# Second tile's normalisation interleaved with the first tile's, in an RWKV block on one core

## The chip, the core and the metric

The kernel runs on one core of one Trainium2 chip. The metric is the device time of one execution in microseconds. A core has engines that each work through their own instructions in order: TensorE (PE, with its weight loads PEld), VectorE (DVE), ScalarE (ACT), GpSimd (POOL) and SyncE (SP). DMA transfers are issued from the queues of SP, ACT and POOL. Engines wait for each other on semaphores.

## The reference

The input x is 2 sequences of 4096 positions with 256 features, float32. The block has two halves, each on a layer norm of x and each added to x:

```python
# attention half (RWKV), on n = layernorm(x); n_prev is n moved by one position
xk, xv, xr = (n * mix + n_prev * (1 - mix) for mix in (mix_k, mix_v, mix_r))
k, v, r = xk @ W_k.T, xv @ W_v.T, sigmoid(xr @ W_r.T)
# a recurrence over positions: running log-max p, numerator q, decay w, bonus u
new_p = max(p, u + k_t)
wkv_t = (exp(p - new_p) * q + exp(u + k_t - new_p) * v_t) / (the two exponentials' sum)
x = x + (r * wkv) @ W_o.T
# feed-forward half, on n = layernorm(x); weights are -1, 0 or 1 with a scale per output
h = silu(n @ w1.T * s1) * (n @ w2.T * s2)
h = gelu(h @ h1.T * sh1)
h = gelu(h @ h2.T * sh2)
x = x + h @ w3.T * s3
```

Layer norm here is (x - mean) / sqrt(variance + 1e-5) over the 256 features.

## The kernel before

Features lie on the 128 partitions, in two halves `h`; positions run along the free axis. A tile is 512 positions, so there are 16 tiles, 8 for each sequence. Tile 0 alone is cut into two pieces of 256 positions (`parts(i)`), so that its steps overlap.

A tile passes through three Python generators, each of which yields between its steps:

- `normalise(i)`: takes the tile's input `x_sb` from `loaded`, starts the load of the next tile on POOL's queue (`load_x`), and runs the first layer norm into `xn`.
- `attention(i)`: mixes `xn` with its neighbour into three tiles `mx`; for each half `h` forms the products `ps_k`, `ps_v`, `ps_r` in PSUM and runs the recurrence `wkv` on VectorE and ScalarE, with the result in `y`; forms the output products `ps_o` and adds them into `x_sb`; runs the second layer norm into `x2`; splits it into a rounded part `x2_hi` and a rest `x2_lo`.
- `ffn(i)`: the feed-forward half. Each product is done twice, with the rounded part and with the rest (`split_product`). The first layer's products are `pa` and `pb`, the next two layers' `ph`, the last one's `po`.

`layernorm` sums the two halves into `both`, takes the mean over partitions with a product against a constant matrix (`average`, into PSUM tile `mean`), subtracts it, squares on ScalarE, takes the variance in the same way (`var`), takes the root on ScalarE and the reciprocal on VectorE, and multiplies. For tile 0 `average` is one float32 product. For the others (`busy`) the sum is first split, with a copy on ScalarE and a subtraction on VectorE into `sums`, and two products are done.

The loops at the end set the order: tile 0 goes through `normalise` and `attention` alone, then `normalise(1)` stands whole; after that the steps of `ffn(i)` are interleaved with those of `attention(i + 1)` and `normalise(i + 2)`:

```python
    run(normalise(0))
    run(attention(0))
    run(normalise(1))
```

A scheduler then orders the instructions of each engine from this; pools give the buffers (`ps_attn` has three PSUM buffers, `ps_sum` one, `ps_ffn` four). ScalarE holds one set of function tables at a time; a change of function can need a table load, which the profile shows as ACT_TABLE_LOAD.

At the start the weights are loaded: `vec` and `wa_sb` (the attention's) on SP's queue, behind half of tile 0's input; the other half of it on ACT's; the feed-forward weights on POOL's, where `w1`, `w2`, `h1`, eight pieces of `h2` (through memory, `h2_hbm`) and `w3` follow each other, and then the input of tile 1. When all tiles are done, a flag decides whether a general version of the block is needed; with these inputs it isn't.

Of the kernel before, what the change touches and what calls it, by code (L numbers as in the profile page):

```python
# [12 lines left out]
P = 128  # L13
B, T, D, HID = 2, 4096, 256, 1024
TS = 512
# [47 lines left out]
def split_block(ctx, tc, flags, x, vecs, w_attn, w1, w2, h1, h2, w3, out):  # L63
# [26 lines left out]

    def load_x(i):
        x_sb = xpool.tile([P, ND, TS], F32, tag="x", name="x_sb")
        for p, queue in zip(parts(i), (nc.sync, nc.scalar) if i == 0 else (nc.gpsimd,)):
            queue.dma_start(out=x_sb[:, :, p], in_=hbm(x, *tiles[i])[:, :, p])
        return x_sb

    loaded = {0: load_x(0)}
    vec = const.tile([P, NVEC], F32, name="vec")
    nc.sync.dma_start(out=vec, in_=vecs)
    wa_sb = const.tile([P, 4, ND, D], F32, name="wa_sb")  # L100
# [11 lines left out]
        nc.gpsimd.dma_start(out=h2_hbm[f], in_=h2[:, :, f * P : (f + 1) * P])  # L112
    nc.gpsimd.dma_start(out=w3_sb, in_=w3)

    mean_w = const.tile([P, P], F32, name="mean_w")
    vector.memset(mean_w, 1.0 / D)
    mean_wr = const.tile([P, P], F32R, name="mean_wr")
    scalar.activation(mean_wr, mean_w, AF.Copy)
    eps = const.tile([P, 1], F32, name="eps")
    vector.memset(eps, LN_EPS)  # L120
    unmix = const.tile([P, 3 * ND], F32, name="unmix")
    vector.tensor_scalar(unmix, vec[:, 0 : 3 * ND], -1.0, 1.0, ALU.mult, ALU.add)

# [30 lines left out]
    def split_product(psum, weights, src):  # L154

        n = len(src)
        for c in range(n):
            hi, lo = src[c]
            tensor.matmul(psum, weights(c), hi, start=c == 0, stop=False)  # L159
            tensor.matmul(psum, weights(c), lo, start=False, stop=c == n - 1)  # L160

    def split(hi, lo, full):

        scalar.activation(hi, full, AF.Copy)  # L164
        vector.tensor_tensor(lo, full, hi.bitcast(F32), ALU.subtract)  # L165

    def average(psum, both, busy):

        if busy:
            pieces = one.tile([P, 2, TS], F32R, tag="sums", name="sums")  # L170
            split(pieces[:, 0, :], pieces[:, 1, :], both)
            split_product(psum, lambda c: mean_wr, [(pieces[:, 0, :], pieces[:, 1, :])])
        else:
            tensor.matmul(psum, mean_w, both, start=True, stop=True)

    def layernorm(src, xc, tag, parts, busy):


        both = one.tile([P, TS], F32, tag=tag, name="both")
        mean = ps_sum.tile([P, TS], F32, tag="ps", name="mean")  # L180
        for p in parts:
            vector.tensor_tensor(both[:, p], src[:, 0, p], src[:, 1, p], ALU.add)
            average(mean[:, p], both[:, p], busy)
        for p in parts:
            for h in range(ND):
                vector.tensor_tensor(xc[:, h, p], src[:, h, p], mean[:, p], ALU.subtract)
        yield
        sq = wide.tile([P, ND, TS], F32, tag="wide", name="sq")
        var = ps_sum.tile([P, TS], F32, tag="ps", name="var")
        rstd = one.tile([P, TS], F32, tag=tag, name="rstd")  # L190
        for p in parts:
            scalar.activation(sq[:, :, p], xc[:, :, p], AF.Square)
            vector.tensor_tensor(sq[:, 0, p], sq[:, 0, p], sq[:, 1, p], ALU.add)
            average(var[:, p], sq[:, 0, p], busy)
        for p in parts:
            scalar.activation(rstd[:, p], var[:, p], AF.Sqrt, bias=eps)  # L196
        yield
        for p in parts:
            vector.reciprocal(rstd[:, p], rstd[:, p])  # L199
            for h in range(ND):  # L200
                vector.tensor_tensor(xc[:, h, p], xc[:, h, p], rstd[:, p], ALU.mult)
        yield

    def wkv(h, k, v, r, y, parts, first):

        w, u = col(DECAY, h), col(FIRST, h)

        lm = one.tile([P, TS + 1], F32, tag="lm", name="lm")
        num = one.tile([P, TS + 1], F32, tag="num", name="num")
        if first:  # L210
            vector.memset(lm[:, 0:1], LOG_ZERO)
            vector.memset(num[:, 0:1], 0.0)  # L212
        else:
            vector.tensor_copy(lm[:, 0:1], log_max[:, h : h + 1])
            vector.tensor_copy(num[:, 0:1], numer[:, h : h + 1])

        def after(p):
            return slice(p.start + 1, p.stop + 1)

        sc = one.tile([P, 2, TS], F32, tag="sc", name="sc")


        so = one.tile([P, 2, TS], F32, tag="so", name="so")
        for p in parts:
            vector.tensor_tensor_scan(
                lm[:, after(p)], w.to_broadcast([P, p.stop - p.start]), k[:, p], lm[:, p.start : p.start + 1],
                ALU.add, ALU.max,
            )  # L230
            vector.scalar_tensor_tensor(sc[:, 1, p], lm[:, p], w, k[:, p], ALU.add, ALU.subtract)
            vector.tensor_scalar(sc[:, 0, p], sc[:, 1, p], NEG_CLAMP, 0.0, ALU.max, ALU.min)
            vector.tensor_scalar(sc[:, 1, p], sc[:, 1, p], 0.0, -NEG_CLAMP, ALU.max, ALU.min)
            scalar.activation(sc[:, 0, p], sc[:, 0, p], AF.Exp)
            scalar.activation(sc[:, 1, p], sc[:, 1, p], AF.Exp, scale=-1.0)
            vector.scalar_tensor_tensor(so[:, 1, p], k[:, p], u, lm[:, p], ALU.add, ALU.subtract)
            vector.tensor_scalar(so[:, 1, p], so[:, 1, p], NEG_CLAMP, -NEG_CLAMP, ALU.max, ALU.min)
        vector.tensor_copy(log_max[:, h : h + 1], lm[:, TS:])
        for p in parts:
            scalar.activation(so[:, 0, p], so[:, 1, p], AF.Sigmoid, scale=-1.0)  # L240
            scalar.activation(so[:, 1, p], so[:, 1, p], AF.Sigmoid)
            scalar.activation(r[:, p], r[:, p], AF.Sigmoid)
        yield
        for p in parts:
            vector.tensor_tensor(sc[:, 1, p], sc[:, 1, p], v[:, p], ALU.mult)
            vector.tensor_tensor_scan(
                num[:, after(p)], sc[:, 0, p], sc[:, 1, p], num[:, p.start : p.start + 1], ALU.mult, ALU.add
            )
        vector.tensor_copy(numer[:, h : h + 1], num[:, TS:])
        yield  # L250
        for p in parts:
            vector.tensor_tensor(so[:, 0, p], so[:, 0, p], num[:, p], ALU.mult)
            vector.tensor_tensor(so[:, 1, p], so[:, 1, p], v[:, p], ALU.mult)
            vector.tensor_tensor(so[:, 0, p], so[:, 0, p], so[:, 1, p], ALU.add)
            vector.tensor_tensor(y[:, h, p], so[:, 0, p], r[:, p], ALU.mult)
        yield
# [3 lines left out]
    def normalise(i):  # L260

        x_sb = loaded.pop(i)
        if i + 1 < len(tiles):
            loaded[i + 1] = load_x(i + 1)

        xn = one.tile([P, ND, TS + 1], F32, tag="xn", name="xn")
        if tiles[i][1] == 0:
            vector.memset(xn[:, :, 0:1], 0.0)
        else:
            vector.tensor_copy(xn[:, :, 0:1], prev)  # L270
        yield from layernorm(x_sb, xn[:, :, 1:], "rstd1", parts(i), i > 0)
        vector.tensor_copy(prev, xn[:, :, TS:])
        normal[i] = (x_sb, xn)

    def attention(i):
# [21 lines left out]
        for h in range(ND):  # L297
            kvr = []
            for m, name in enumerate("kvr"):
                ps = ps_attn.tile([P, TS], F32, tag="pa", name="ps_" + name)  # L300
                for p in ps_of:
                    product(
                        ps[:, p],
                        lambda c, m=m: wa_sb[:, m, c, h * P : (h + 1) * P],
                        [mixed[m][:, c, p] for c in range(ND)],
                    )
                kvr.append(ps)
            yield
            yield from wkv(h, *kvr, y, ps_of, first)

        for h in range(ND):
            ps = ps_attn.tile([P, TS], F32, tag="pa", name="ps_o")
            for p in ps_of:
# [4 lines left out]
                )  # L318
                vector.tensor_tensor(x_sb[:, h, p], x_sb[:, h, p], ps[:, p], ALU.add)
        yield  # L320
        x2 = wide.tile([P, ND, TS], F32, tag="wide", name="x2")
        yield from layernorm(x_sb, x2, "rstd2", ps_of, i > 0)
        x2_hi = one.tile([P, ND, TS], F32R, tag="x2_hi", name="x2_hi")
        x2_lo = one.tile([P, ND, TS], F32R, tag="x2_lo", name="x2_lo")
        for p in ps_of:
# [58 lines left out]
        for _ in steps:  # L384
            pass

    normal, got = {}, {}
    run(normalise(0))
    run(attention(0))
    run(normalise(1))  # L390
    for i in range(len(tiles)):
        ahead = attention(i + 1) if i + 1 < len(tiles) else iter(())
        further = normalise(i + 2) if i + 2 < len(tiles) else iter(())
        for step, _ in enumerate(ffn(i, *got.pop(i))):

            if step >= NH:
                next(ahead, None)
            if step > 2 * NH - 2 and step % 2:
                next(further, None)
        run(ahead)  # L400
        run(further)
# [287 lines left out]
```

## Time and profile before

| | |
|---|---|
| runs, device us | 1613.01, 1613.53, 1614.44; median 1613.53 |
| profiled execution, device us | 1613.69 |
| its span | 1611.9 us |
| around the span | 1.8 us |
| mean granted TensorE clock | 0.993 |
| busy: PE / DVE / ACT / POOL | 1571.8 / 1077.4 / 1014.0 / 58.4 us |

The profile records one execution. "Busy" is the time in which an engine has an instruction in work; a row of the timeline gives an instruction's start and length in microseconds, its engine, its line in the kernel, what it writes and reads, and in brackets how long the engine had stood idle before it and what it then had waited for. The clock is the share of TensorE's full speed that was granted. A line can be that of a helper: all split products have lines 159 and 160, all plain products 152.

### The profile page before, as it was taken

To read this page: it belongs to the slowest core of one execution; us is meant where nothing else is said; L and a number is where in the kernel's file an instruction comes from. 1 tells how busy PE (TensorE), PEld (TensorE's weight loads), DVE (VectorE), ACT (ScalarE), POOL (GpSimd) and SP (SyncE) were. 2 spreads that over 40 slices of the span, in tenths; PEclk is the share of its full clock that TensorE was granted. 3 is DMA by queue.
4 is the path that set the end of the run, shared out by engine and by line. 5 is a ranking of instruction groups with operands and counts; after the bars stand their busy time and mean duration, and the time that the engine had idled before them with its cause. 6 is when DMAs were issued, how large, how long until landed. Compare 5 with 4: busy or idle time off the path is not lost.

```text
span 1611.9 us, 16567 instructions
## 1 busy us (share of the span) xinstructions
PE 1571.8 (98%) x6314; PEld 1189.0 (74%) x6314; DVE 1077.4 (67%) x1746; ACT 1014.0 (63%) x1351; POOL 58.4 (4%) x91
## 2 busy tenths in 40 slices
PE   4799999999999999999999999999999999999997
PEld 3577778777777777777777777777778777787786
DVE  7767667585766958668585676857668575675521
ACT  6566666766657567576666657667576666657542
POOL 2000000000000000000000000000000000000000
PEclk9899999999999999999999999999999999999999
DMA  9003122130311203113030221203112031110202
GB/s 366 26 1 105 40 79 72 33 116 15 105 53 53 92 14 118 39 52 99 19 119 27 78 72 43 96 13 102 43 53 85 7 105 40 65 59 34 91 9 72
DMA packets 36230, 109.16 MB, mean 68 GB/s; under 512 B 3632, under 2 KB 12336, under 8 KB 35504
## 3 DMA queue, kind: packets, MB, share of 16 engines
q1 hardware_dynamic: 18992, 68.45, 13.0%
q0 software_dynamic: 16880, 39.33, 7.9%
q8 instruction: 51, 0.84, 0.2%
q14 instruction: 35, 0.29, 0.1%
q10 hardware_dynamic: 272, 0.26, 0.0%
HBM read 99.64 MB, written 12.58 MB: 70 GB/s over the span
## 4 chain that ended last, share of the span: by engine, by line
PE 79%; issue 15%; DMA 3%; DVE 1%; ACT 1%; POOL 0%; POOLq 0%; ACTq 0%
PE ph L159 24%; PE ph L160 24%; PE pa L159 3%; PE pa L160 3%; PE pb L159 3%; PE pb L160 3%; PE po L159 3%; PE po L160 3%; PE ps_o L152 3%; PE ps_v L152 3%; PE ps_r L152 3%; PE ps_k L152 3%; DMA h_hbm<-in_h 1%; DMA x_sb<-in_x 1%; PE mean L159 0%
## 5 line engine op out<-in xcount | busy, mean ns | idle before, releaser
L159 PE MATMUL ph<-hi,h_sb 128*128 128x512 f32 x2048 | 817.2, 399 | 0.3 <-DMA h_sb<-h_hbm 0.3
L160 PE MATMUL ph<-lo,h_sb 128*128 128x512 f32 x2048 | 803.7, 393 | 0.0
L159 PEld LDWEIGHTS ph<-hi,h_sb 128*128 128x128 f32 x2048 | 384.6, 188 | 95.4 <-issue 7.4
L160 PEld LDWEIGHTS ph<-lo,h_sb 128*128 128x128 f32 x2048 | 385.0, 188 | 90.8 <-issue 7.2
L365 DVE TENSOR_TENSOR lo<-full,hi 128x512 fp32r<-128x512 f32 x256 | 175.3, 685 | 321.7 <-ACT full L364 321.6
L362 ACT ACTIVATE hi<-ph,vec 128x512 fp32r<-128x512 f32 x256 | 176.0, 687 | 295.5 <-PE ph L160 294.4
L364 ACT ACTIVATE full<-ph,vec 128x512 f32<-128x512 f32 x256 | 174.3, 681 | 0.0
L362 ACT ACT_TABLE_LOAD x102 | 130.9, 1283 | 1.8
L346 ACT ACTIVATE gated<-pa,vec 128x512 f32<-128x512 f32 x128 | 86.9, 683 | 63.5 <-PE pa L160 62.3
L347 DVE SCALAR_TENSOR_TENSOR gated<-pb,vec,gated 128x512 f32<-128x512 f32 x128 | 95.4, 748 | 31.3 <-PE pb L160 21.9
L199 DVE RECIPROCAL rstd<-rstd 128x512 f32<-128x512 f32 (+1 forms) x34 | 107.2, 3158 | 6.9 <-ACT rstd L196 6.9
L159 PE MATMUL pa<-x_hi,w_sb 128*128 128x512 f32 x256 | 104.5, 408 | 4.5 <-ACT x_hi L164 3.8
L160 PE MATMUL pa<-x_lo,w_sb 128*128 128x512 f32 x256 | 104.5, 408 | 0.0
L159 PE MATMUL pb<-x_hi,w_sb 128*128 128x512 f32 x256 | 102.3, 400 | 0.0
L160 PE MATMUL pb<-x_lo,w_sb 128*128 128x512 f32 x256 | 101.5, 396 | 0.0
L164 ACT ACTIVATE hi<-gated 128x512 fp32r<-128x512 f32 x128 | 80.2, 628 | 33.1 <-DVE gated L347 31.5
L159 PE MATMUL po<-hi,w_sb 128*128 128x512 f32 x256 | 99.5, 398 | 0.0
L160 PE MATMUL po<-lo,w_sb 128*128 128x512 f32 x256 | 98.6, 394 | 0.0
L165 DVE TENSOR_TENSOR lo<-gated,hi 128x512 fp32r<-128x512 f32 x128 | 87.6, 686 | 12.2 <-ACT hi L164 9.1
L289 DVE SCALAR_TENSOR_TENSOR mx<-xn,vec,mx 128x512 f32<-128x512 f32 (+1 forms) x102 | 71.3, 716 | 0.4
L152 PE MATMUL ps_k<-mx,wa_sb 128*128 128x512 f32 (+1 forms) x136 | 63.3, 584 | 5.9 <-DVE mx L289 5.6
L152 PE MATMUL ps_v<-mx,wa_sb 128*128 128x512 f32 (+1 forms) x136 | 63.0, 590 | 5.0 <-DVE num L212 5.0
(101 smaller groups left out, 1699.4 us busy)
## 6 DMA issues: line engine op xcount, KB each, us to landing
h_sb<-h_hbm SPq DMA_DIRECT2D x128, 512.0 KB, 3.3
out<-x_sb POOLq DMA_DIRECT2D x16, 512.0 KB, 3.1
raw<-in_h POOLq DMA_DIRECT2D x32, 256.0 KB, 3.1
x_sb<-in_x POOLq DMA_DIRECT2D x15, 512.0 KB, 4.1
h_sb<-in_h POOLq DMA_DIRECT2D x1, 4096.0 KB, 19.8
h_hbm<-in_h POOLq DMA_DIRECT2D x8, 512.0 KB, 23.4
w_sb<-in_w POOLq DMA_DIRECT2D x3, 1024.0 KB, 10.6
raw<-in_w POOLq DMA_DIRECT2D x12, 256.0 KB, 2.8
```

The lines of the kernel that those rows point to most:

```text
L152: tensor.matmul(psum, weights(c), src[c], start=c == 0, stop=c == n - 1)
L159: tensor.matmul(psum, weights(c), hi, start=c == 0, stop=False)
L160: tensor.matmul(psum, weights(c), lo, start=False, stop=c == n - 1)
L164: scalar.activation(hi, full, AF.Copy)
L165: vector.tensor_tensor(lo, full, hi.bitcast(F32), ALU.subtract)
L199: vector.reciprocal(rstd[:, p], rstd[:, p])
L289: vector.scalar_tensor_tensor(mx[:, h, p], xn[:, h, p.start + 1 : p.stop + 1], vec[:, j : j + 1], mx[:, h, p], ALU.mult, ALU.add,)
L346: scalar.activation(full, pa, AF.Silu, scale=col(S1, f))
L347: vector.scalar_tensor_tensor(full, pb, col(S2, f), full, ALU.mult, ALU.mult)
L362: scalar.activation(hi, ps, AF.Gelu, scale=col(scales, f))
L364: scalar.activation(full, ps, AF.Gelu, scale=col(scales, f))
L365: vector.tensor_tensor(lo, full, hi.bitcast(F32), ALU.subtract)
```

## The change

It has six parts.

1. Tile 1's input is issued at the start, on ACT's queue behind the second half of tile 0's input; before, `normalise(0)` issued it on POOL's queue, behind the weights.
2. `layernorm` is cut in two: `column_mean` makes `both` and the mean, `layernorm` the rest. The split, the sums and the products leave their last instruction in `marks`.
3. `normalise(1)` is no longer run whole after tile 0's attention. Its mean is computed between tile 0's first variance and its root. Its subtraction and square stand around tile 0's second root, and the rest runs with the odd steps of `ffn(0)`. `tc.issue_after(ins)` ties the instructions made inside it behind `ins` where both are on one engine; it adds an order, and no wait for another engine.
4. A root of one element (`load_sqrt_table`) at the start, and one behind tile 0's last sigmoid, make ScalarE load the root's table at these places.
5. Tile 1's mean lies in a buffer of `ps_ffn`, since it is held from tile 0's first norm to its second.
6. `ps_k` and `ps_v` of tile 0's second half take buffers of `ps_ffn` too; `ps_r` stays in `ps_attn`.

The diff, cut to its core:

```diff
-        for p, queue in zip(parts(i), (nc.sync, nc.scalar) if i == 0 else (nc.gpsimd,)):
+        queues = {0: (nc.sync, nc.scalar), 1: (nc.scalar,)}.get(i, (nc.gpsimd,))
+        for p, queue in zip(parts(i), queues):
             queue.dma_start(out=x_sb[:, :, p], in_=hbm(x, *tiles[i])[:, :, p])
...
-    loaded = {0: load_x(0)}
+    loaded = {i: load_x(i) for i in range(2)}
...
+    def load_sqrt_table():
+        return scalar.activation(root, eps, AF.Sqrt)
+
+    load_sqrt_table()
...
     def split(hi, lo, full):
-        scalar.activation(hi, full, AF.Copy)
-        vector.tensor_tensor(lo, full, hi.bitcast(F32), ALU.subtract)
+        marks["high"] = scalar.activation(hi, full, AF.Copy)
+        marks["split"] = vector.tensor_tensor(lo, full, hi.bitcast(F32), ALU.subtract)
...
+    def column_mean(src, mean, tag, parts, busy, pause=False):
+        if pause:
+            both = tmp.tile([P, TS], F32, tag="full", name="both")
         else:
-            tensor.matmul(psum, mean_w, both, start=True, stop=True)
-
-    def layernorm(src, xc, tag, parts, busy):
-        both = one.tile([P, TS], F32, tag=tag, name="both")
-        mean = ps_sum.tile([P, TS], F32, tag="ps", name="mean")
-        for p in parts:
-            vector.tensor_tensor(both[:, p], src[:, 0, p], src[:, 1, p], ALU.add)
-            average(mean[:, p], both[:, p], busy)
+            both = one.tile([P, TS], F32, tag=tag, name="both")
+        for p in parts:
+            marks["both"] = vector.tensor_tensor(both[:, p], src[:, 0, p], src[:, 1, p], ALU.add)
+            if pause:
+                yield
+            marks["mean"] = average(mean[:, p], both[:, p], busy)
+
+    def layernorm(src, mean, xc, tag, parts, busy, pause=False):
...
-            vector.tensor_tensor(sq[:, 0, p], sq[:, 0, p], sq[:, 1, p], ALU.add)
-            average(var[:, p], sq[:, 0, p], busy)
+            marks["sq"] = vector.tensor_tensor(sq[:, 0, p], sq[:, 0, p], sq[:, 1, p], ALU.add)
+            marks["var"] = average(var[:, p], sq[:, 0, p], busy)
+        if pause:
+            yield
...
     def normalise(i):
         x_sb = loaded.pop(i)
-        if i + 1 < len(tiles):
+        if i + 1 < len(tiles) and i > 0:
             loaded[i + 1] = load_x(i + 1)
+
+        pool, tag = (ps_ffn, "pf") if i == 1 else (ps_sum, "ps")
+        mean = pool.tile([P, TS], F32, tag=tag, name="mean")
+        yield from column_mean(x_sb, mean, "rstd1", parts(i), i > 0, i == 1)
+        if i == 1:
+            yield
...
-                ps = ps_attn.tile([P, TS], F32, tag="pa", name="ps_" + name)
+                pool, tag = (ps_ffn, "pf") if i == 0 and h and name != "r" else (ps_attn, "pa")
+                ps = pool.tile([P, TS], F32, tag=tag, name="ps_" + name)
...
+        if i == 0:
+            with tc.issue_after(marks["sigmoid"].ins):
+                load_sqrt_table()
...
-    run(normalise(0))
-    run(attention(0))
-    run(normalise(1))
+    here, second = normalise(0), normalise(1)
+    for _ in range(2):
+        next(here)
+    with tc.issue_after(marks["sq"].ins):
+        next(second)
+        next(second)
+    with tc.issue_after(marks["split"].ins), tc.issue_after(marks["high"].ins):
+        run(here)
+    here = attention(0)
+    for _ in range(3 + 4 * ND + 3):
+        next(here)
+    with tc.issue_after(marks["sq"].ins):
+        next(second)
+    run(here)
+    with tc.issue_after(marks["split"].ins):
+        next(second)
...
             if step >= NH:
                 next(ahead, None)
+            if i == 0 and step % 2:
+                next(second, None)
```

In the program that results, VectorE has tile 1's `both` and `sums` between tile 0's second sum of squares and its first reciprocal, and tile 1's two subtractions between the sums of squares and the reciprocals of tile 0's second norm. ScalarE has the copy for `sums` ahead of tile 0's first root, and tile 1's square ahead of `x2_hi`. TensorE has tile 1's two mean products ahead of the first `ps_k`. From `ffn(0)`'s second layer on, the order of all engines is the old one but for a few neighbouring VectorE instructions.

More of the change, by code (lines that the diff above doesn't have):

```diff
@@ L113, in split_block @@
     nc.gpsimd.dma_start(out=w3_sb, in_=w3)
+    eps = const.tile([P, 1], F32, name="eps")
+    vector.memset(eps, LN_EPS)
+    root = const.tile([P, 1], F32, name="root")
+    def load_sqrt_table():
+        return scalar.activation(root, eps, AF.Sqrt)
+    load_sqrt_table()
     mean_w = const.tile([P, P], F32, name="mean_w")
@@ L118, in split_block @@
     scalar.activation(mean_wr, mean_w, AF.Copy)
-    eps = const.tile([P, 1], F32, name="eps")
-    vector.memset(eps, LN_EPS)
     unmix = const.tile([P, 3 * ND], F32, name="unmix")
@@ L159, in split_product @@
             tensor.matmul(psum, weights(c), hi, start=c == 0, stop=False)
-            tensor.matmul(psum, weights(c), lo, start=False, stop=c == n - 1)
+            last = tensor.matmul(psum, weights(c), lo, start=False, stop=c == n - 1)
+        return last
     def split(hi, lo, full):
-        scalar.activation(hi, full, AF.Copy)
-        vector.tensor_tensor(lo, full, hi.bitcast(F32), ALU.subtract)
+        marks["high"] = scalar.activation(hi, full, AF.Copy)
+        marks["split"] = vector.tensor_tensor(lo, full, hi.bitcast(F32), ALU.subtract)
     def average(psum, both, busy):
@@ L171, in average @@
             split(pieces[:, 0, :], pieces[:, 1, :], both)
-            split_product(psum, lambda c: mean_wr, [(pieces[:, 0, :], pieces[:, 1, :])])
-        else:
-            tensor.matmul(psum, mean_w, both, start=True, stop=True)
-    def layernorm(src, xc, tag, parts, busy):
-        both = one.tile([P, TS], F32, tag=tag, name="both")
-        mean = ps_sum.tile([P, TS], F32, tag="ps", name="mean")
+            return split_product(psum, lambda c: mean_wr, [(pieces[:, 0, :], pieces[:, 1, :])])
+        return tensor.matmul(psum, mean_w, both, start=True, stop=True)
+    def column_mean(src, mean, tag, parts, busy, pause=False):
+        if pause:
+            both = tmp.tile([P, TS], F32, tag="full", name="both")
+        else:
+            both = one.tile([P, TS], F32, tag=tag, name="both")
         for p in parts:
-            vector.tensor_tensor(both[:, p], src[:, 0, p], src[:, 1, p], ALU.add)
-            average(mean[:, p], both[:, p], busy)
+            marks["both"] = vector.tensor_tensor(both[:, p], src[:, 0, p], src[:, 1, p], ALU.add)
[3 more added lines that the diff above has]
+    def layernorm(src, mean, xc, tag, parts, busy, pause=False):
         for p in parts:
@@ L240, in wkv @@
             scalar.activation(so[:, 0, p], so[:, 1, p], AF.Sigmoid, scale=-1.0)
-            scalar.activation(so[:, 1, p], so[:, 1, p], AF.Sigmoid)
+            marks["sigmoid"] = scalar.activation(so[:, 1, p], so[:, 1, p], AF.Sigmoid)
             scalar.activation(r[:, p], r[:, p], AF.Sigmoid)
@@ L270, in normalise @@
             vector.tensor_copy(xn[:, :, 0:1], prev)
-        yield from layernorm(x_sb, xn[:, :, 1:], "rstd1", parts(i), i > 0)
+        yield from layernorm(x_sb, mean, xn[:, :, 1:], "rstd1", parts(i), i > 0, i == 0)
         vector.tensor_copy(prev, xn[:, :, TS:])
@@ L320, in attention @@
         yield
+        if i == 0:
+            with tc.issue_after(marks["sigmoid"].ins):
+                load_sqrt_table()
+        mean = ps_sum.tile([P, TS], F32, tag="ps", name="mean")
+        yield from column_mean(x_sb, mean, "rstd2", ps_of, i > 0)
         x2 = wide.tile([P, ND, TS], F32, tag="wide", name="x2")
-        yield from layernorm(x_sb, x2, "rstd2", ps_of, i > 0)
+        yield from layernorm(x_sb, mean, x2, "rstd2", ps_of, i > 0, i == 0)
         x2_hi = one.tile([P, ND, TS], F32R, tag="x2_hi", name="x2_hi")
@@ L385, in run @@
             pass
-    normal, got = {}, {}
-    run(normalise(0))
-    run(attention(0))
-    run(normalise(1))
+    normal, got, marks = {}, {}, {}
+    here, second = normalise(0), normalise(1)
[14 more added lines that the diff above has]
+        next(second)
     for i in range(len(tiles)):
```

## The prediction

> **What bounds the kernel now.** I read the page first (busy shares and the 40 slices), then the busy time by stage, then the order of instructions in the first 80 us, then the granted clock and the DMA queues in narrow stretches.
>
> ```profile
> span 1611.9 us, 16567 instructions
> PE 1571.8 (98%) x6314; PEld 1189.0 (74%) x6314; DVE 1077.4 (67%) x1746; ACT 1014.0 (63%) x1351; POOL 58.4 (4%) x91
> PE   4799999999999999999999999999999999999997
> ```
>
> TensorE is busy for 98% and only the first two slices and the last have room. By stage (columns: stretch, its length, then busy us of PE, PEld, DVE, ACT, POOL; clock; DMA share; GB/s):
>
> ```profile
> 0.00:20.00 20.00, 7.30 (x16) 4.83 (x17) 11.57 (x31) 9.54 (x19) 7.23 (x14) 1.00 0.96 380
> 20.00:40.00 20.00, 12.84 (x44) 9.81 (x42) 19.15 (x56) 17.67 (x29) 2.84 (x4) 0.91 1.66 351
> 40.00:60.00 20.00, 10.49 (x29) 6.15 (x30) 14.46 (x30) 5.81 (x9) 0.00 (x0) 0.74 0.15 57
> 60.00:80.00 20.00, 19.21 (x74) 14.31 (x73) 16.40 (x23) 16.16 (x23) 0.00 (x0) 0.92 0.01 1
> 80.00:100.00 20.00, 20.00 (x77) 14.29 (x76) 14.95 (x29) 9.67 (x14) 0.00 (x0) 1.00 0.00 1
> ```
>
> From 80 us TensorE never stops, and the changed program's order there is the old one but for three small VectorE swaps. So the whole change is decided before the first `ph` product (77.65 us in the trace): a microsecond won or lost there is one won or lost at the end. The places that it touches:
>
> ```profile
> 11.76 3.36 DVE L199 RECIPROCAL rstd<-rstd 128x256 f32<-128x256 f32 x2 [2.01 <-ACT rstd L196]
> 32.32 3.53 PE L152 MATMUL ps_v<-mx,wa_sb 128*128 128x256 f32 x8 [5.04 <-DVE num L212]
> 42.72 0.69 DVE L182 TENSOR_TENSOR both<-x_sb 128x512 f32<-128x512 f32 x1 [1.78 <-DMA x_sb<-in_x]
> 43.99 0.42 DVE L255 TENSOR_TENSOR y<-so,ps_r 128x256 f32<-128x256 f32 x1
> 44.13 1.99 PE L152 MATMUL ps_o<-y,wa_sb 128*128 128x256 f32 x8 [1.91 <-DVE x_sb L319]
> 49.93 1.28 ACT L196 ACT_TABLE_LOAD   x1
> 51.88 0.84 ACT L196 ACTIVATE rstd<-var,eps 128x256 f32<-128x256 f32 x2 [0.66 <-PE var L174]
> ```
>
> VectorE, in order, stood 1.78 us at 42.72 for the second tile's input while the first tile's last `y` waited behind it.
>
> **The change part by part.**
>
> *Square root table ahead: 0.* Both loads (1.28 us at 9.31 and at 49.93) end 0.66 us before the root starts; the root waits for the `var` product. Cover: 2.07 us of `var`. The Trainium skill (ScalarE: Activation LUTs, "What ACT_TABLE_LOAD costs") counts 1.28 us of load plus a drain of 1.38 for each switch; by it the loads would end at 11.97 and 52.59, after the products, and the change would gain 0.7 us twice. In the trace the load at 60.53 takes 1.28 us and the Silu behind it starts at 61.83: no drain. The trace decides: 0, not -1.4. The two 1-element roots hide in ScalarE's idle time (2.54 to 8.00, and after 40).
>
> *The mean of tile 1 in the gap before the reciprocal: 0 if the data is there.* The added run is `both` 0.69 (VectorE), `sums` copy 0.63 (ScalarE), `sums` rest 0.69 (VectorE): 2.01 us with hand-overs inside, in a gap of 2.01 us (9.74 to 11.76). The reciprocal keeps its 11.76, and the two mean products stand on TensorE where it idles until 16.85. But `both` now stands in VectorE's line ahead of the first tile's reciprocal, ScalarE's copy ahead of its root: if tile 1's input lands at L later than 9.7, everything is L - 9.7 later.
>
> *When does it land?* It was issued behind all weights on POOL's queue (25.78, landing 42.7); now it is ScalarE's second transfer, issued near 1.25, behind the first tile's half, which landed at 4.9. How queues share the engines the trace shows twice, for 6.0 to 9.5 us (packets of 8 KB in both) and 28.5 to 32.5 us (4 KB against 512 bytes):
>
> ```profile
> q1 hardware_dynamic: 96, 0.79, 55.1%
> q0 software_dynamic: 97, 0.66, 47.1%
> ...
> q1 hardware_dynamic: 342, 1.27, 87.4%
> q0 software_dynamic: 444, 0.23, 29.1%
> ```
>
> Nearly packet by packet, not by bytes. An 8 KB packet costs an engine about 0.32 us (3.5 us x 16 / 177 packets), one of 4 KB 0.17 (from 40.5 to 42.5 us two inputs flow alone: 32 / 189). The input is 512 KB, 128 packets of 4 KB, 8 for each engine. Against the w1/w2 stream alone a round is 0.49, with `wa_sb` as third 0.81. `wa_sb`'s 8 rounds of 0.65 ended about 10.4 (it landed at 10.94), so it began near 5.2. Start 4.5, two rounds alone, six of 0.81: 10.4, and 0.4 to 1.0 for completion: L = 10.8 to 11.4. I take 11.2: +1.5 us. Bounds: equal bytes (8.5, nothing lost) and last of all (14.5). `wa_sb` in turn comes 1.3 us or more later, near 12.5; it is needed at 16.85. POOL's queue is rid of one transfer, and tile 2's input comes sooner; nobody waits for it.
>
> *The wait at 42.72 goes: -2.5.* Out of VectorE's line ahead of the last `y` go 1.78 idle, 0.61 for `both` and 0.33 for a residual sum that now stands behind; 0.2 returns for a copy that moved ahead. The stage before is VectorE's (19.15 of 20), so giving `ps_k`/`ps_v` of the second half their own PSUM buffers (the 5.04 us wait at 32.32) moves TensorE's work forward and shortens nothing by itself.
>
> *What that early work does to the clock: +1.9.* This is the rule against the change. The clock by stretches of 3.41 us:
>
> ```profile
> 29.18:32.59 3.41, 0.27 (x1) 0.27 (x2) 3.31 (x12) 3.37 (x8) 0.00 (x0) 1.00 1.16 373
> 32.59:36.00 3.41, 3.41 (x9) 2.68 (x9) 3.33 (x11) 2.95 (x4) 0.00 (x0) 0.50 1.74 360
> 46.24:49.66 3.42, 1.33 (x4) 0.53 (x4) 2.60 (x8) 1.01 (x2) 0.00 (x0) 1.00 0.00 0
> 49.66:53.07 3.41, 2.38 (x5) 1.44 (x6) 1.16 (x3) 2.37 (x4) 0.00 (x0) 0.50 0.00 0
> ```
>
> After a stretch with little TensorE work the next runs at half clock, after a full one at full. The Trainium skill (TensorE: Matmul & The Clock Gate, "The HAM clock gate") says the same of windows of about 3.4 us that run free of the kernel. Before, `ps_v` and `ps_r` at 32.3 to 37.5 warmed the clock just ahead of the output products (16 instructions at 0.24 us at 44.13). After, those products are done by about 31 and TensorE has two small pieces of `ps_o` until 40.4: at least one empty window. So `ps_o` runs at 0.43 us an instruction, as `ps_v` did at 32.32 (3.53 for 8). Four calls of two instructions follow the last `y`, 8 x 0.19 = 1.5, and part of a call before it plus a longer tail, up to 1.0: with a cold clock to the end 2.5, with a warm one 0. A window border within them turns it warm; I take 1.9. By the trace's time without the rule this part would be 0 and the sum -2.1.
>
> *FFN of tile 0: -1.1.* The stage from the first `pa` (57.74) to the first `ph` (77.65) lasts 19.9. It has 66 products: 15.4 at 0.2335, 2.5 more for 13 at half clock, so 2.0 of stalls. Two `xn` subtractions (0.6 each of VectorE's time, at 56.94 and 58.74) and the 1.06 us square on ScalarE at 59.46 leave this stage for idle time at 50.4 to 52.4 (VectorE) and 52.7 to 56.4 (ScalarE). `x_lo` no longer stands behind a subtraction (0.35 at 58.88), gating starts 0.8 sooner after `pa`, the 3.35 us reciprocal near 3 us sooner. Following the new order instruction by instruction with the old durations gives 18.8. What stays are the switch to the root's table and back and the reciprocal: late next.
>
> *Sum:* +1.5 - 2.5 + 1.9 - 1.1 = -0.2 us. The profiled execution took 1613.69 (span 1611.9 and 1.8 around it), so 1613.5; it stands 0.16 above the median of the runs, 1613.53, so the median goes to 1613.3.
>
> **The rivals.**
>
> *The gain in full.* The input lands by 9.7 and the clock is warm at `ps_o`: 0 - 2.5 + 0 - 1.1 = -3.6, at 1609.9; on time with the cold clock -1.7 to -2.1, at 1611.6. For it: the first halves took only 4 us to land. Against: the packet turns above, and the idle hole at 31 to 40, which I see no way to fill.
>
> *The input is last (slower).* Place: VectorE's `both` ahead of the first reciprocal. If ScalarE's second transfer gets no packets until `wa_sb` is through (near 9.9), it has 8 rounds of 0.49 to go and 0.6 for completion: L = 14.5, +4.8 instead of +1.5, so +3.1, 1616.6, and more for each round lost. It decides from L of about 14.6. For it: `wa_sb`, third on its queue, began 3.5 us after its issue. Against: the two hardware queues moved the halves of the first input together.
>
> *It does nothing.* The 1.78 us wait is hidden by something: against it, `y` at 43.99 is what `ps_o` needs.
>
> **How the numbers follow.** Within 0.2% is 3.2 us, about what a measurement of this kernel can tell from no change. The likeliest case (L 10.3 to 12.7, part of the clock lost) spans -1.5 to +1.7, 1612.0 to 1615.2: chance 0.57. On time: 0.20, of which 0.09 beyond -3.2. Late: 0.20, of which 0.14 beyond +3.2. Nothing: 0.03. Faster 0.09, same 0.77, slower 0.14. The range leaves out the fastest of the on-time and the latest of the late cases: 1610.9 to 1616.4.
>
> **What would show it.** `both` of tile 1 waits 1 to 2 us for its DMA near 11; the first reciprocal starts near 13.2 in place of 11.76; the wait at 42.72 is gone; half clock at `ps_o` near 42; both roots wait for `var`; first `pa` to first `ph` about 18.8. A landing before 9.7 or after 14, or full clock at `ps_o`, would prove the sum wrong.

## The result, and the profile after

The changed kernel takes 1611.14 us (median of 19 runs, 1608.28 to 1613.94), the kernel before 1613.42 beside it (19 runs, 1612.12 to 1615.17): ratio 0.9986, 95% interval 0.9979 to 0.9992. That is 2.3 us or 0.14% less, within what the forecast called "the same" and inside its range: 2.2 us below its likeliest value and 0.2 us above the range's lower end. The runs of the changed kernel spread over 5.7 us, those of before over 3.1.

The profiled execution has a span of 1608.9 us and took 1610.68. The page's first lines:

```profile
span 1608.9 us, 16567 instructions
PE 1571.1 (98%) x6314; PEld 1188.8 (74%) x6314; DVE 1077.3 (67%) x1746; ACT 1013.8 (63%) x1352; POOL 57.6 (4%) x90
PE   5799999999999999999999999999999999999997
```

Busy time did not change; what changed is where TensorE stands in the first two slices. By stage (columns as in the table of before):

```profile
0.00:20.00 20.00, 8.99 (x18) 5.71 (x19) 13.38 (x33) 9.30 (x20) 7.23 (x14) 1.00 0.95 376
20.00:40.00 20.00, 11.49 (x47) 9.00 (x47) 19.12 (x58) 18.30 (x30) 2.03 (x3) 0.87 1.61 359
40.00:60.00 20.00, 11.65 (x27) 7.36 (x26) 14.07 (x27) 7.00 (x12) 0.00 (x0) 0.59 0.14 54
60.00:80.00 20.00, 19.68 (x80) 15.22 (x80) 17.62 (x26) 14.85 (x21) 0.00 (x0) 0.95 0.00 0
```

The clock of 40 to 60 us fell from 0.74 to 0.59. The timeline at the places that the change touches:

```profile
9.34 0.68 DVE L191 TENSOR_TENSOR both<-x_sb 128x512 f32<-128x512 f32 x1
10.93 0.84 ACT L212 ACTIVATE rstd<-var,eps 128x256 f32<-128x256 f32 x2 [0.24 <-PE var L181]
11.44 3.37 DVE L215 RECIPROCAL rstd<-rstd 128x256 f32<-128x256 f32 x2
25.78 1.89 PE L159 MATMUL ps_v<-mx,wa_sb 128*128 128x256 f32 x8
40.41 0.42 DVE L271 TENSOR_TENSOR y<-so,ps_r 128x256 f32<-128x256 f32 x1
39.30 5.70 PE L159 MATMUL ps_o<-y,wa_sb 128*128 128x256 f32 x12 [6.34 <-DVE y L271]
45.03 0.42 DVE L343 TENSOR_TENSOR x_sb<-x_sb,ps_o 128x256 f32<-128x256 f32 x1 [1.29 <-PE ps_o L159]
50.75 0.84 ACT L212 ACTIVATE rstd<-var,eps 128x256 f32<-128x256 f32 x2 [1.96 <-PE var L181]
```

Tile 1's `both` (VectorE's sum of the tile's two halves) stands at 9.34 and has no bracket: its input was there. The wait at 42.72 is gone and the last `y` comes at 40.41 instead of 43.99. Then `ps_o`, which took 1.99 us for its last 8 instructions, takes 5.70 for 12, and now VectorE waits for it (1.29). The clock rows go with it: TensorE is empty from 33 to 39 and the grant falls.

```profile
33.00:36.00 3.00, 0.00 (x0) 0.00 (x0) 3.00 (x11) 2.93 (x6) 0.00 (x0) 0.79 1.63 357
36.00:39.00 3.00, 0.00 (x0) 0.00 (x0) 2.46 (x9) 2.93 (x6) 0.00 (x0) 0.50 2.04 354
39.00:42.00 3.00, 2.70 (x6) 1.87 (x7) 2.68 (x9) 1.69 (x3) 0.00 (x0) 0.50 1.11 411
42.00:45.00 3.00, 3.00 (x9) 2.37 (x8) 0.71 (x2) 0.00 (x0) 0.00 (x0) 0.50 0.20 82
```

In the kernel before, the last of these stretches had full clock:

```profile
42.00:45.00 3.00, 1.09 (x6) 0.79 (x5) 2.28 (x6) 0.63 (x1) 0.00 (x0) 1.00 0.32 119
```

So the lead over the kernel before is 3.6 us at the last `y`, 1.1 at the first `pa` (57.74 to 56.6) and 2.1 at the first `ph` (77.65 to 75.5).

### The profile page after: what moved, and what is told of

The parts are those of the page before. It is cut to its first block, busy times and chain, and to the rows that moved or that the text cites. A ratio compares the mean times of both kernels' runs of the same rounds, so it can differ in the third digit from the quotient of the medians.

```text
span 1608.9 us, 16567 instructions
## 1 busy us (share of the span) xinstructions
PE 1571.1 (98%) x6314; PEld 1188.8 (74%) x6314; DVE 1077.3 (67%) x1746; ACT 1013.8 (63%) x1352; POOL 57.6 (4%) x90
## 4 chain that ended last, share of the span: by engine, by line
PE 80%; issue 15%; DVE 2%; ACT 1%; DMA 0%; POOL 0%; POOLq 0%; ACTq 0%
PE ph L167 24%; PE ph L166 24%; PE ps_o L159 3%; PE pa L166 3%; PE pb L167 3%; PE pa L167 3%; PE pb L166 3%; PE po L167 3%; PE po L166 3%; PE ps_r L159 3%; PE ps_v L159 3%; PE ps_k L159 3%; DVE rstd L215 0%; PE mean L166 0%; PE mean L167 0%
## 5 line engine op out<-in xcount | busy, mean ns | idle before, releaser
L159 PE MATMUL ps_o<-y,wa_sb 128*128 128x512 f32 (+1 forms) x136 | 61.2, 593 | 8.5 <-DVE y L271 6.6
```

The lines of the kernel that those rows point to most:

```text
L159: tensor.matmul(psum, weights(c), src[c], start=c == 0, stop=c == n - 1)
```

## The experiments

Each ran beside the kernel before on the same chip, in groups of four (e1 to e4, e5 to e8, e9 to e12); across groups the ratios compare better than the times.

| kernel | median us | runs from, to | ratio to before | 95% interval |
|---|---|---|---|---|
| changed kernel | 1611.14 | 1608.28, 1613.94 | 0.9986 | 0.9979, 0.9992 |
| e1 late input | 1623.66 | 1622.97, 1625.14 | 1.0062 | 1.0048, 1.0075 |
| e2 input alone | 1611.12 | 1609.99, 1612.23 | 0.9982 | 0.9974, 0.9990 |
| e3 no own banks | 1609.40 | 1608.23, 1613.71 | 0.9980 | 0.9970, 0.9989 |
| e4 no table loads | 1611.75 | 1610.16, 1615.83 | 0.9988 | 0.9981, 0.9994 |
| e5 20 fillers at `ps_o` | 1611.22 | 1608.59, 1614.41 | 0.9983 | 0.9975, 0.9992 |
| e6 e3, 16 fillers ahead of the FFN | 1609.89 | 1608.07, 1614.85 | 0.9983 | 0.9976, 0.9989 |
| e7 e3, input in halves | 1611.59 | 1610.54, 1618.32 | 0.9993 | 0.9987, 1.0000 |
| e8 e6 and e7 | 1612.96 | 1610.43, 1616.91 | 0.9993 | 0.9985, 1.0001 |
| e9 32 fillers at `ps_o` | 1607.96 | 1607.58, 1610.24 | 0.9958 | 0.9945, 0.9972 |
| e10 e3, input first on POOL's queue | 1610.88 | 1609.76, 1613.01 | 0.9978 | 0.9969, 0.9987 |
| e11 e10, root ahead of Silu | 1610.13 | 1608.99, 1611.24 | 0.9972 | 0.9961, 0.9983 |
| e12 e11, 16 fillers | 1608.22 | 1607.92, 1608.86 | 0.9960 | 0.9946, 0.9973 |

**e1_late_input: does a late landing cost one for one?**

```diff
-        queues = {0: (nc.sync, nc.scalar), 1: (nc.scalar,)}.get(i, (nc.gpsimd,))
+        queues = {0: (nc.sync, nc.scalar), 1: (nc.sync,)}.get(i, (nc.gpsimd,))
...
     nc.sync.dma_start(out=wa_sb, in_=w_attn)
+    loaded[1] = load_x(1)
```

> The changed kernel with the second tile's input issued on SyncE's queue behind wa_sb instead of as ScalarE's second transfer; nothing else differs. Theory (the prediction's landing rule was right, only its size wrong: whatever the input is late beyond about 9.7 us is lost one for one, because `both` of tile 1 stands in VectorE's line ahead of the first reciprocal): the input lands after wa_sb, at 12.5 to 14.5; `both` waits 3 to 5 us for its DMA, the first reciprocal starts at 14.5 to 16.5 in place of 11.44, the first ps_k (a first product that also needs wa_sb) moves later by the same, and the time is 1.5 to 5 us above the changed kernel, so 1612.5 to 1616. Rival (the input's landing is not what decides; there is slack in front of the first ps_k or the time is won elsewhere): within 0.5 us of the changed kernel, near 1611.

Far slower than either foresaw: the input landed 21.1 us after its issue, near 23.3. The timeline of VectorE:

```profile
23.30 0.69 DVE L192 TENSOR_TENSOR both<-x_sb 128x512 f32<-128x512 f32 x1 [13.94 <-DMA x_sb<-in_x]
25.30 3.36 DVE L216 RECIPROCAL rstd<-rstd 128x256 f32<-128x256 f32 x2
54.51 0.42 DVE L272 TENSOR_TENSOR y<-so,ps_r 128x256 f32<-128x256 f32 x1
```

The reciprocal is 13.9 us later than in the changed kernel, the last `y` 14.1, the whole 12.5. One for one up to `y` is shown; behind it this execution won 1.7 back (14.5 us from the last `y` to the first `pa` instead of 16.2; 12 instructions of `ps_o` took 4.72 us instead of 5.70). Why so late, the DMA queues from 11 to 16 us say (packets, MB, share of the engines):

```profile
q0 software_dynamic: 101, 2.20, 104.0%
q1 hardware_dynamic: 100, 0.20, 12.0%
```

100 packets of the input for 101 of POOL's stream: turn by turn, though POOL's carry eleven times the bytes. The transfer in small packets beside a stream in large ones got the share of its packets' number.

**e2_input_alone: what is one part worth?** The kernel before, with the first part of the change alone.

```diff
+        queues = {0: (nc.sync, nc.scalar), 1: (nc.scalar,)}.get(i, (nc.gpsimd,))
...
-    loaded = {0: load_x(0)}
+    loaded = {i: load_x(i) for i in range(2)}
...
-        if i + 1 < len(tiles):
+        if i + 1 < len(tiles) and i > 0:
```

> The kernel before with one part of the change alone: the second tile's input as ScalarE's second transfer at the start instead of behind all weights on GpSimd's queue. Order of all products, of VectorE and of ScalarE as before. Theory (what is won is the 1.78 us that VectorE stood at 42.72; the interleaving wins at ps_o but cools the clock): the wait at 42.72 is gone, the ps_o products stay warm because ps_v and ps_r at 32 to 37 still run just ahead of them, the first pa comes about 2 us sooner, the stage from first pa to first ph stays near 19.9, and the whole is 1.8 to 2.2 us faster than before: about 1611.3, the same as the full change. Rival (the interleaving and the own banks do the work): 0.5 us or less faster than before, the wait at 42.72 is taken over by another.

As the theory had it, to 0.2 us. The wait at 42.72 is gone, `both` runs at 21.88 and waits for nothing, and `ps_o` is warm, as TensorE's timeline has it:

```profile
33.48 3.78 PE L153 MATMUL ps_v<-mx,wa_sb 128*128 128x256 f32 x8 [4.71 <-DVE num L213]
41.92 3.29 PE L153 MATMUL ps_o<-y,wa_sb 128*128 128x256 f32 x14 [2.38 <-DVE y L256]
```

Its 1611.12 is the full change's 1611.14: everything else in the change adds up to nothing that these runs can tell. Its runs spread over 2.2 us.

**e3_no_own_banks: does the early work cool the clock?**

```diff
-                pool, tag = (ps_ffn, "pf") if i == 0 and h and name != "r" else (ps_attn, "pa")
-                ps = pool.tile([P, TS], F32, tag=tag, name="ps_" + name)
+                ps = ps_attn.tile([P, TS], F32, tag="pa", name="ps_" + name)
```

> The changed kernel, with ps_k and ps_v of the second half of tile 0 back in the three shared PSUM buffers, so that they wait for the first half's as before. Theory (the early products leave TensorE empty from 31 to 40 and so cool the clock for ps_o): products of ps_v and ps_r run again at 30 to 36, the clock at ps_o near 40 is full in most runs, ps_o is done about 1 to 2 us sooner, and the time is 0.5 to 1.5 us below the changed kernel: 1609.6 to 1610.6. Rival (early products help, a clock cost does not exist or lies elsewhere): equal to or slower than the changed kernel, by up to 1 us.

Its 1609.4 is 0.2 below the range. `ps_v` stands late again and `ps_o` is warm:

```profile
32.00 3.55 PE L159 MATMUL ps_v<-mx,wa_sb 128*128 128x256 f32 x8 [5.04 <-DVE num L228]
40.34 3.29 PE L159 MATMUL ps_o<-y,wa_sb 128*128 128x256 f32 x14 [2.64 <-DVE y L271]
54.54 0.79 PE L166 MATMUL pa<-x_hi,w_sb 128*128 128x512 f32 x1 [5.90 <-ACT x_hi L172]
```

From the last `y` (41.42) to the first `pa` it is 13.1 us; in the changed kernel 16.2. Counted from the first `both`, the last `y` comes after 36.9 us here, 36.1 in the changed kernel. So in this pair of executions the own banks win 0.75 at `y` and lose 3.1 behind it. The loss is not the same in every execution: e10 below, without own banks too, lost most of it. The intervals of the two kernels' times overlap, so the times only agree.

**e4_no_table: do the table loads matter?**

```diff
-    load_sqrt_table()
     mean_w = const.tile([P, P], F32, name="mean_w")
...
-        if i == 0:
-            with tc.issue_after(marks["sigmoid"].ins):
-                load_sqrt_table()
```

> The changed kernel without the two 1-element square roots that load the square root table ahead. Theory (the loads of 1.28 us end before the var products do): both roots still wait for var, the table loads stand in front of them as in the kernel before, difference to the changed kernel under 0.3 us. Rival (a switch costs a load and a drain, 2.7 us, more than the cover): each root 0.7 us later, time 0.7 to 1.4 us above the changed kernel, 1611.8 to 1612.5.

The time is 0.6 above the changed kernel's, and the intervals overlap. ScalarE's timeline contradicts both theories at the first root:

```profile
13.39 0.63 ACT L171 ACTIVATE sums<-both 128x512 fp32r<-128x512 f32 x1 [4.22 <-DVE both L190]
14.04 1.28 ACT L211 ACT_TABLE_LOAD   x1
15.33 0.84 ACT L211 ACTIVATE rstd<-var,eps 128x256 f32<-128x256 f32 x2
```

The load now stands behind the copy for tile 1's `sums`, and VectorE's reciprocal waited 1.09 for the root. So in the new order loading ahead is worth about 1 us, which only keeps what the old order had for nothing. No drain follows the load (it ends at 15.32, the root starts at 15.33), so the 2.7 us of the rival, the count that the prediction quotes, are not met. At the second root (53.95) the load ended with the products, and nothing was lost.

More was in VectorE's timeline of this execution:

```profile
12.66 0.69 DVE L190 TENSOR_TENSOR both<-x_sb 128x512 f32<-128x512 f32 x1 [3.04 <-DMA x_sb<-in_x]
```

With the changed kernel's own queues the input came 11.4 us after its issue, where it had taken 6.6. The queues in the second from 9 to 10 us, while the last packets (q10, ScalarE's queue) came through:

```profile
q1 hardware_dynamic: 27, 0.22, 54.7%
q0 software_dynamic: 25, 0.20, 48.7%
q10 hardware_dynamic: 2, 0.00, 1.1%
```

One or two packets a microsecond, between two streams of 8 KB packets. From 6 us to the landing q10 has ten packets in all. This fits one DMA engine with that many left when the streams began; which engines they were was not looked at.

**e5_warm_o and e9_warm_o32: `ps_o` with the clock kept warm.** The changed kernel, with products that nobody reads behind the last `ps_r` of tile 0; 20 in e5, 32 in e9.

```diff
+    def keep_warm(n, behind):
+        filler = ps_ffn.tile([P, TS], F32, tag="pf", name="filler")
+        with tc.issue_after(behind.ins):
+            for _ in range(n):
+                tensor.matmul(filler, mean_wr, w1_sb[:, 0, 0:TS], start=True, stop=True)
...
+            if i == 0 and h:
+                keep_warm(32, marks["product"])
```

> The changed kernel with 20 filler products (128x512, their result is read by nobody, 0.2335 us each at full clock) on TensorE behind the last ps_r product of tile 0, in the stretch from 33 to 39 us that is empty in the changed kernel. Theory (the early products of the change leave a hole that cools the clock, and ps_o pays for it): in the profile the granted clock at 39 to 45 us is 1.00 instead of 0.50, the 12 ps_o instructions behind the last y take near 3 us instead of 5.70, from the last y to the first pa is 13 to 14 us instead of 16.2, and the time is 1 to 2.5 us below the changed kernel: 1608.6 to 1610.1. Rival (the clock is not what made that stage longer; VectorE's added work is): the stage stays at 16, the time within 0.5 of the changed kernel.

> As e5, with 32 filler products instead of 20: in e5 the fillers ended at 36.3, the next stretch was empty again and ps_o ran at half clock all the same (5.69 us for 12), so e5 did not test the clock. 32 of them at 0.2335 us end near 39, just ahead of the last y when the input lands on time. Theory (half clock at ps_o costs the changed kernel 1.9 to 3 us): clock 1.00 from 39 to 45 us, the last pieces of ps_o at 0.24 us an instruction, last y to first pa 13 to 14 us instead of 16.1 to 16.2, time 1 to 2 us below the changed kernel (1611.1): 1609 to 1610. Rival (VectorE sets that stage): 16 us again and 1611.

e5 did not reach `ps_o`: the fillers ended at 36.3, one stretch later the clock was down and `ps_o` took 5.69 for 12 again. e9 is the test. Its clock:

```profile
36.00:39.00 3.00, 3.00 (x15) 2.40 (x14) 2.94 (x11) 2.92 (x7) 0.00 (x0) 1.00 1.92 349
39.00:42.00 3.00, 1.29 (x7) 0.79 (x5) 2.52 (x8) 2.92 (x6) 0.00 (x0) 1.00 1.45 401
42.00:45.00 3.00, 2.92 (x11) 1.98 (x12) 2.38 (x9) 1.36 (x2) 0.00 (x0) 1.00 0.50 197
```

and its timeline:

```profile
43.69 0.41 DVE L277 TENSOR_TENSOR y<-so,ps_r 128x256 f32<-128x256 f32 x1
31.55 7.82 PE L159 MATMUL filler<-w_sb,mean_wr 128*128 128x512 f32 x32
41.95 3.44 PE L165 MATMUL ps_o<-y,wa_sb 128*128 128x256 f32 x12 [1.71 <-DVE y L277]
```

12 instructions in 3.44 instead of 5.70, and 12.6 us from the last `y` to the first `pa` (56.3) instead of 16.2. The median is 1607.96, ratio 0.9958 against 0.9986 for the changed kernel, and the intervals do not touch. So 7.5 us of products for nothing (32 at 0.2335) make the kernel faster, by 3.2 us by the medians and more by the ratios, since before took 1614.31 in this group. The theory had asked for 1 to 2. The trace agrees: from tile 1's `both`, which leaves the late landing out, the first `pa` comes after 44.2 us in e9 and 47.3 in the changed kernel. With its input 2.5 us late, the profiled execution (1610.24) is the slowest of e9's five.

**e6_warm_ffn: the FFN's start with a warm clock.** On e3, with `keep_warm` as above:

```diff
+        if pause and tag == "rstd2":
+            keep_warm(16, marks["var"])
         if pause:
             yield
```

> The kernel without own banks (e3) with 16 filler products between the second var of tile 0 and its first pa, where TensorE is empty for 5.9 us and the clock falls to half just ahead of the FFN. Theory (the first dozen FFN products run at half clock in all kernels so far, 0.427 instead of 0.2335 each): clock 1.00 at the first pa, first pa to first ph about 16.5 to 17.5 us instead of 18.9, time 1 to 2.5 us below e3: 1607 to 1608.4. Rival (the stalls of that stage on ScalarE and VectorE take up whatever TensorE wins): the first products are fast but first pa to first ph stays within 0.5 of 18.9.

It is the rival that came. The first products run at full clock and TensorE is through with what it has at 60.65; then its timeline shows:

```profile
62.90 0.65 PE L172 MATMUL pa<-x_hi,w_sb 128*128 128x512 f32 x1 [2.25 <-ACT gated L382]
```

It waits for ScalarE's gating. ScalarE's timeline at that place holds, between the first Silu and the second, the switch to the root's table, tile 1's root and the switch back:

```profile
57.65 0.69 ACT L382 ACTIVATE gated<-pa,vec 128x512 f32<-128x512 f32 x1
58.35 1.28 ACT L220 ACT_TABLE_LOAD   x1
59.65 0.69 ACT L220 ACTIVATE rstd<-var,eps 128x512 f32<-128x512 f32 x1
60.87 1.28 ACT L382 ACT_TABLE_LOAD   x1
62.16 1.26 ACT L382 ACTIVATE gated<-pa,vec 128x512 f32<-128x512 f32 x2
```

From the first `pa` to the first `ph` it is 19.7 us, in e3 18.9: TensorE's early lead was spent waiting, and after the wait the clock was down again (0.52 from 63 to 66).

**e7_early and e8_early_warm_ffn: the input in two halves.** On e3 and on e6.

```diff
-        queues = {0: (nc.sync, nc.scalar), 1: (nc.scalar,)}.get(i, (nc.gpsimd,))
-        for p, queue in zip(parts(i), queues):
+        queues = (nc.sync, nc.scalar) if i < 2 else (nc.gpsimd,)
+        for p, queue in zip(parts(0) if i < 2 else parts(i), queues):
```

> The kernel without own banks (e3) with the second tile's input in two halves, one on SyncE's and one on ScalarE's queue, right behind the first tile's halves, instead of whole on ScalarE's. Theory (in some executions a few packets of the input are left when the weights' streams of 8 KB packets begin near 5.3 us, and wait their turn behind them: it landed at 7.85, 9.45 and 12.6 in three profiled executions with the same queues, and what lies beyond 9.4 is paid): the halves are through sooner, `both` never waits for its DMA, the spread of the runs shrinks from 5.5 us to 3 or less, the upper end falls from 1613.7 to 1611 or less, and the median falls by 0 to 1 us. wa_sb lands later, by up to 1.5 us, which nobody waits for. Rival (the spread is the clock's free-running windows): spread and median as e3, 1609.4.

> e6 and e7 together: no own banks, input early in two halves, 16 filler products ahead of the FFN. Theory: the gains add, 1606.5 to 1608, about 6 us (0.4%) below the kernel before and 3 to 4 below the changed one. Rival: no better than e3, 1609.4.

Both slower than e3 and e6, by a fault of the experiment: `vec` now stood behind the input on SP's queue, and VectorE's `unmix`, in line ahead of everything, waited for it:

```profile
10.24 0.25 DVE L129 TENSOR_SCALAR unmix<-vec 128x6 f32<-128x6 f32 x1 [5.14 <-DMA vec<-in_vecs]
```

About the landing they say nothing. A transfer of 22 KB that nobody had thought of cost more than the one that was to be helped.

**e10_pool_head: the input first on POOL's queue.**

```diff
-        queues = {0: (nc.sync, nc.scalar), 1: (nc.scalar,)}.get(i, (nc.gpsimd,))
+        queues = (nc.sync, nc.scalar) if i == 0 else (nc.gpsimd,)
```

> The kernel without own banks (e3) with the second tile's input on GpSimd's queue, as in the kernel before, but first in it, ahead of all weights, instead of on ScalarE's. (e7 missed its point: `vec` came behind the input and `unmix` held up VectorE for 5.1 us.) Theory (on ScalarE's queue the last few packets of 2 KB take turns with two streams of 8 KB packets and land anywhere from 7.85 to 12.6; first on GpSimd's queue, w1 stands behind the input and only wa_sb takes turns with it): the input lands at 7 to 9.5 each time, `both` does not wait, the spread of the runs shrinks from e3's 5.5 us to 3 or less, median 1608.5 to 1609.5. Rival (the spread is the clock's): spread 5 us, median 1609.4; rival two (GpSimd's queue starts later than ScalarE's and the input lands at 10 to 11): a wait of 1 us or so in `both` and 1610.5.

The second rival: `both` waited 1.52 for its DMA, and 1.51 and 1.50 in the profiles of e11 and e12, which have the same queues. It is late each time, and equally late; the median is 1.5 above e3's (the intervals overlap), and the runs spread over 3.3 us instead of e3's 5.5.

The profiled execution, the slowest of the eleven (1613.01), also lost the clock at `ps_o`, without own banks; TensorE's timeline and the clock:

```profile
41.75 4.98 PE L159 MATMUL ps_o<-y,wa_sb 128*128 128x256 f32 x14 [2.79 <-DVE y L271]
42.00:45.00 3.00, 3.00 (x11) 2.42 (x11) 2.08 (x7) 0.56 (x2) 0.00 (x0) 0.68 0.25 101
```

14 instructions in 4.98 where e3 took 3.29, and 15.5 us from the last `y` to the first `pa`. e8 shows the same (4.98 and 15.5); e3, e6, e7, e11 and e12, in the same order up to there, took 3.29 and 13.1. TensorE had stood idle for 2.79 and 2.77 us ahead of these `ps_o` in the two, for 2.64 or less in the five. So the mean of the seven is 13.8; the three profiles with own banks and no fillers have 16.2, 15.0 (e4) and 14.5 (e1), mean 15.2. The own banks' loss is 1.4 us by these means, not e3's 3.1.

**e11_root_first and e12_root_first_warm: one switch of tables less.** On e10; e12 with the 16 fillers of e6.

```diff
+            if i == 0 and f == 0:
+                with tc.issue_after(marks["root"].ins):
+                    scalar.activation(full, pa, AF.Silu, scale=col(S1, f))
...
-    run(here)
-    with tc.issue_after(marks["split"].ins):
+    for _ in range(2):
+        next(here)
+    with tc.issue_after(marks["scaled"].ins):
         next(second)
+    with tc.issue_after(marks["sq"].ins):
+        run(here)
```

> e10, and in the second tile's first normalisation its squares' sum stands ahead of tile 0's x_lo on VectorE and its square root ahead of the first Silu on ScalarE: two table loads of 1.28 us (Silu, square root, Silu becomes square root, Silu) go, and the 3.35 us reciprocal starts some 3 us sooner. Theory (e6 showed that with a warm clock TensorE only ran ahead and then stood 2.25 us for `gated`: ScalarE's switch of tables and the reciprocal are what sets the stage from first pa to first ph): that stage takes 17.5 to 18.2 us instead of 18.9 and the time is 0.7 to 1.4 us below e10. Rival (another wait, for PSUM or for x_lo 0.7 us later, takes the place): within 0.3 of e10.

> e11 with the 16 filler products of e6 ahead of the FFN. Theory (with the switch of tables out of the way the clock at the start of the FFN counts): first pa to first ph 15.7 to 17 us, time 1 to 2 us below e11, so 1606 to 1607.5, 6 us below the kernel before. Rival (the stage is bound by ScalarE and VectorE even so): as e11.

Both as the theory had it, but that e12's 1608.22 is above the 1606 to 1607.5 it named. ScalarE's timeline of e12, where e6 had a load ahead of the first Silu and the two shown:

```profile
58.47 0.69 ACT L220 ACTIVATE rstd<-var,eps 128x512 f32<-128x512 f32 x1 [1.84 <-PE var L173]
59.17 1.28 ACT L384 ACT_TABLE_LOAD   x1
60.47 0.69 ACT L384 ACTIVATE gated<-pa,vec 128x512 f32<-128x512 f32 x1
```

First `pa` to first `ph` is 18.9 us in e10, 17.8 in e11, 16.7 in e12, and the times fall by 0.75 and 1.9. The first of these steps rests on the trace (the runs of e10 and e11 overlap); all five runs of e12 lie below all seven of e11. The same fillers that won nothing in e6 win here: at this place the clock counts only when the switch of tables is out of the way. e12, at 0.9960, and e9, at 0.9958, beat both kernels. The two together, with the input on ScalarE's queue, were not run.

## Why the prediction was right, and where it was off

The shape was right: the wait at 42.72 goes, the early products cool the clock, and most of the gain is given back at `ps_o`. What happened is the rival "on time with the cold clock", which stood at 1611.6. The measured time lies below the 1612.0 to 1615.2 of the likeliest case and only 0.24 us inside the range: the late landing of that case did not come in the profiled execution. By its own steps, on the profiled execution:

*Square root table ahead: 0.* Right: both roots waited for `var` (0.24 and 1.96 us). e4 adds that the calls are needed in the new order: without them VectorE waited 1.1 us for the first root.

*Landing of tile 1's input: +1.5; measured 0.* This is the step that failed, by its size. L, the time of landing, was taken as 11.2; the input landed near 7.9. The prediction let it begin at 4.5 in 128 packets of 4 KB, six of eight rounds in turns with two streams. In the trace it came in packets of 2 KB (q10 moved 0.53 MB more than in e1, in 272 packets more; in the kernel before, that queue had moved its half of tile 0 in 272 packets for 0.26 MB, so small packets could have been expected) and most were through before the streams began, as the row for 4 to 5 us has it:

```profile
q10 hardware_dynamic: 187, 0.37, 99.6%
q1 hardware_dynamic: 49, 0.01, 4.7%
```

POOL's stream has no packet in that microsecond; in the kernel before it had 45. Why it began later stays open. Taking turns decides only over the last few packets. But the term is no fixed 0 either. In the six profiled executions with this order of queues and this place of `both`, the input came in time three times (the changed kernel, e3, e6) and 2.17, 2.52 and 3.04 us late three times (e5, e9, e4): 1.3 us in the mean. That this is near the +1.5 is luck: what was forecast was a steady turn-taking over six rounds, and not a tail of a few packets. e1 shows that such a delay goes through to `y` in full. The timed runs have no trace, so that the wide spread of such kernels (5.5 to 6.8 us for the changed kernel, e3, e4, e5 and e6, where e2, in which the landing doesn't matter, has 2.2; e9, of five runs, has 2.7) comes from this is argued, not shown. The range also grows with the number of runs: the kernel before has 4.8 us over 40 runs and 5.3 over 57. And the clock is a rival: in e10, whose landing was the same in the three profiles of its queue order, one execution lost 2.4 us at `ps_o` by the clock alone (15.5 us against 13.1). e3's ten runs lie in two groups, 1608.2 to 1609.4 and 1612.7 to 1613.7; their distance of about 4 us is more than the latest landing, 3.04, explains by itself, and which executions had what stays open.

*The wait at 42.72: -2.5.* Right: from the first `both` to the last `y` it was 39.4 us before and 36.9 in e3, which has no own banks. *Own banks "shorten nothing by itself"*: wrong by 0.75, the 36.9 became 36.1.

*Clock at `ps_o`: +1.9; measured +2.45* (last `y` to first `pa` 13.75 before, 16.2 after). The prediction's "16 instructions" at 44.13 are 8 in its row, which changes nothing. The rule that the prediction weighed against the change (the Trainium skill, TensorE: Matmul & The Clock Gate, "The HAM clock gate") is borne out: an empty stretch, then half clock (in e10 and e8 a stretch with 1.33 and 1.38 us of work in 3.41 was enough), and with the stretch filled (e9) full clock at the same place. Left out, this part would have been 0. Against the profiles without own banks it is 3.1 where these kept the clock (five of seven) and 0.7 where they lost it in part (e8, e10).

*FFN of tile 0: -1.1; measured -1.0* (19.9 to 18.9). e6, e11 and e12 show what is late next, as the prediction said: the switch of tables and the reciprocal.

*Sum* to the first `ph`: 0 - 2.5 - 0.75 + 2.45 - 1.0 = -1.8, and 0.3 because tile 0's own input landed sooner (first `both` 4.62 to 4.30): -2.1, as measured. From there to the end the trace gains 0.9 more, of which 0.3 is one wait in the kernel before (a `ph` product for `h_sb`); the rest stays open. So the two profiled executions differ by 3.0 us, the medians by 2.3. Of the other rivals, the gain in full, the input last of all and no effect, none came; e1 shows what the second would have cost for each microsecond.

## What to carry to other kernels

Moving work earlier leaves a hole where it was. Here TensorE's clock fell in the hole, and the next burst paid for it (12 instructions in 5.70 us instead of 3.44). So look at what ran just ahead of the critical products; if no useful work can fill the hole, products for nothing may be worth their place. A change of many parts should be split on the chip: here one part of the six, alone, brought as much as all of them. And ask of each transfer what it takes turns with: with a few small packets left beside two streams of large ones, programs with the same queues had their input at 7.9 or at 12.6.

## What the runs showed of the hardware that was not expected

The share that a queue gets went by packets to the last: 100 against 101 in 5 us, at 0.20 MB against 2.20 (e1). The same three queues, issued in the same order, landed the same 512 KB anywhere from 6.4 (e2) to 11.4 us (e4) after the issue, while a place at the head of POOL's queue gave 9.0, 9.1 and 9.0. And keeping TensorE busy until 4 us ahead of a burst did not keep its clock (e5: busy to 37.3, `ps_o` at 41.4, clock 0.81 from 39 to 42 and 0.50 after); keeping it busy until 2 us ahead did (e9: busy to 40.2, `ps_o` at 41.95, clock 1.00). Between them the place of the hole seems to decide, though the size of the hole (2.77 us and more, 2.64 and less) sorts these runs the same way. Counted in stretches of 3.41 us, as in the prediction, and placed by where the clock changes in the same trace: TensorE was busy for 1.33 us (e10, from 39.67), 1.38 (e8, from 41.83) and 1.40 (changed kernel, from 31.33) in a stretch ahead of half clock, and for 1.64 (e3, from 38.57) and 1.70 (e11, from 40.17) in one at the same place ahead of full clock.
